# Layer 0, mixing weights: where the stride lies, in the matmul's read or in the copy's write

## Chip, cores, metric

The kernel runs on one core of one Trainium2 chip. The metric is device microseconds of one execution of the whole program; the reported time is the median of three executions.

## What is computed

The program is a chain of four layers on an image batch of 8 x 64 channels x 64 x 64. The change touches layer 0 alone, a spectral mixing layer (cut from the reference):

```python
z  = layernorm over channels(x) * ln_gamma + ln_beta
Xf = rfft2(z)                                             # 64 x 33 frequencies
Uf = Xf[:, :, None] * conj(phi_f)[None, None]             # 24 filters phi
U  = irfft2(Uf)
S  = einsum('bdlxy,lhd->bhxy', U, theta)
V  = einsum('hd,bdxy->bhxy', wv, S) + bv
G  = sigmoid(einsum('hd,bdxy->bhxy', wg, S) + bg)
return x + V * G
```

Filtering and the sum over filters and channels commute with the inverse transform. So the kernel forms, for every frequency, one mixing matrix from phi and theta, applies it to the spectrum, and transforms back once. Layers 1 to 3 (selective scans and convolutions) are the same before and after.

## The kernel before

Layer 0 runs in three stages, one after the other: `l0_forward` (normalise, transform along y), `l0_mix` (transform along x, mix, transform back along x) and `l0_back` (transform back along y, gate, add). Layer 1 follows. Inside the layer the order of work is the order of the code: each engine executes its own instructions in program order, and semaphores hold an instruction until its data or its buffer is ready.

`l0_mix` goes through the 33 values of ky in 17 pairs (the last pair holds one). For a pair there is one tile of mixing weights, `W`, of 128 partitions; partitions 0 to 63 multiply the real part of the input channels and 64 to 127 the imaginary part. Two such tiles exist, so the weights of the next pair are made while the present pair is applied. Four helpers share the work:

- `build(p)` makes `W` of pair p in 16 steps. A step runs four matmuls (line 692) into the two-bank PSUM tile `pw`, one for each of four output channels h; each gives 256 columns: two ky, real and imaginary (c), 64 values of kx. Then `evac` (lines 299 and 301) copies the 1024 columns out of PSUM. `evac` alternates: one copy on VectorE (line 299), the next on ScalarE (line 301), through all of its callers. There are two `pw` buffers, so the third step waits until the copy of the first has finished.
- `spectrum(p)` loads the input of a ky from DRAM (`yt`, line 708), transforms it (line 711, PSUM tile `q`) and scatters it into `xf` with two ScalarE and two VectorE instructions that take turns (lines 729 and 727). `xf` has kx outside and the batch inside, so that 8 columns of one kx lie together.
- `apply(p)` does the mixing. For each ky there are two halves of 32 kx each. A half is 32 matmuls (line 742) into the PSUM tile `ps`, of which there is one buffer. Four neighbouring kx go to four column tiles of the array, each 32 columns wide, and so to four groups of 32 PSUM partitions. The stationary operand is `xf` of that kx, the moving operand the 128 weights of that kx (2 c x 64 h). Then one `evac` to `so` and eight DMAs to DRAM (line 754).
- `inverse` transforms a finished ky back along x (line 766), with an `evac` to `o` and a DMA (line 769).

After each half of `apply` the code runs four steps of `build` for the next pair. So PE's order within a pair is: line 711 for the next pair, then four times (32 matmuls of line 742, then 16 matmuls of line 692), then line 766. A float32 matmul shows as two records in the trace: 64 records of line 742 in a half, and 8 of line 692 in a step.

The two accesses that the change swaps are the copy's output and the matmul's moving operand:

```python
W[p] = wp.tile([128, C, n], F32, name="W")                                  # h outside, (ky c kx) inside
o = W[p][:, 4 * m : 4 * m + 4, :].rearrange("p (r e) n -> p r (e n)", r=2)  # copy: contiguous
w = W[p].rearrange("p h (e c x) -> p e c h x", c=2, x=HW)[:, e]             # w[:, :, :, kx]: step n = 256 elements
```

Of the kernel before, what the change touches and what calls it, by code (L numbers as in the profile page):

```python
# [10 lines left out]
F32 = mybir.dt.float32  # L11
# [7 lines left out]
C = 64  # L19
HW = 64  # L20
# [248 lines left out]
class Net:  # L269
# [397 lines left out]
    def l0_mix(self, cp, wp, hy, hm, hs):  # L667

        nc, d = self.nc, self.d
        W2 = NB * C
        theta, phi, xdft, xinv, g, b = (self.load(cp, "l0_" + n) for n in ("theta", "phi", "xdft", "xinv", "g", "b"))
        for r in range(2):
            nc.scalar.mul(phi[r * 64 : r * 64 + NLAG, :, 1, :], phi[r * 64 : r * 64 + NLAG, :, 1, :], -1.0)

        nc.scalar.mul(b, b, float(L))
        pairs = [list(range(k, min(k + 2, KY))) for k in range(0, KY, 2)]
        W, xf, s2 = {}, {}, {}  # L680

        def build(p, pw_):

            kys = pairs[p]
            n = len(kys) * 2 * HW
            W[p] = wp.tile([128, C, n], F32, name="W")
            for m in range(C // 4):
                pw = pw_.tile([128, 2, 512], F32, name="pw")
                for e in range(2):
                    for r in range(2):  # L690
                        at = slice(r * 64, r * 64 + 2 * NLAG)
                        nc.tensor.matmul(
                            pw[:, r, e * n : e * n + n],
                            theta[at, 2 * m + e, :],
                            phi[at, kys[0] : kys[-1] + 1].rearrange("p k c x -> p (k c x)"),
                            start=True,
                            stop=True,
                        )
                o = W[p][:, 4 * m : 4 * m + 4, :].rearrange("p (r e) n -> p r (e n)", r=2)
                self.evac(o, pw[:, :, : 2 * n])  # L700
                yield

        def spectrum(p):

            for ky in pairs[p]:
                k, v = (ky % 32, 0 if ky % 32 else 1 + ky // 32)
                yt = tp.tile([128, W2], F32, name="yt")
                nc.sync.dma_start(yt, hy[k].rearrange("x s n -> (x s) n"))
                px = pq.tile([128, NP, 2, HW], F32, name="q")
                for q in range(NP):  # L710
                    nc.tensor.matmul(
                        px[:, q].rearrange("p c x -> p (c x)"),
                        yt[:, q * 128 : q * 128 + 128],
                        xdft[:, v].rearrange("p c x -> p (c x)"),
                        start=True,
                        stop=True,
                    )

                xf[ky] = tp.tile([128, (HW + 3) * NB], F32, name="xf", bufs=5)
                x = xf[ky].rearrange("p (x b) -> p b x", b=NB)  # L720
                nc.gpsimd.memset(x[:, :, HW:], 0.0)  # L721
                for i in range(2):
                    for c in range(2):
                        o = x[c * C : c * C + C, :, :HW].rearrange("p (q i) x -> p q i x", i=2)[:, :, i, :]
                        src_, scale = px[i * C : i * C + C, :, c, :], g[i * C : i * C + C]
                        if c:
                            nc.vector.tensor_scalar(o, src_, scale, None, ALU.mult)
                        else:
                            nc.scalar.activation(o, src_, AF.Copy, scale=scale)
                if ky == 0:  # L730
                    nc.vector.tensor_scalar(x[:C, :, 0], x[:C, :, 0], b[:C], None, ALU.add)

        def apply(p):
            for e, ky in enumerate(pairs[p]):
                w = W[p].rearrange("p h (e c x) -> p e c h x", c=2, x=HW)[:, e]
                x = xf.pop(ky)
                for half in range(2):
                    ps = ps_.tile([128, 8, 2, C], F32, name="ps")
                    for m in range(8):
                        for j in range(4):  # L740
                            kx = 4 * (half * 8 + m) + j
                            nc.tensor.matmul(  # L742
                                ps[32 * j : 32 * j + 32, m],
                                x[:, kx * NB : kx * NB + 32],
                                w[:, :, :, kx],
                                start=True,
                                stop=True,
                            )
                    so = tp.tile([128, 8, 2, C], F32, name="so")
                    self.evac(so, ps)  # L750
                    for j in range(4):
                        for c in range(2):
                            o = hm[ky, c].rearrange("(m j) b h -> j b m h", j=4)[j, :, half * 8 : half * 8 + 8, :]
                            nc.sync.dma_start(o, so[32 * j : 32 * j + NB, :, c, :])
                    yield

        def fetch(ky):
            s2[ky] = tp.tile([128, W2], F32, name="s2", bufs=4)
            nc.sync.dma_start(s2[ky], hm[ky].rearrange("c x b h -> (c x) (b h)"))

        def inverse(kys):

            po = pq.tile([128, W2], F32, name="q")
            for n, ky in enumerate(kys):
                v = 0 if ky % 32 else 1 + ky // 32
                nc.tensor.matmul(po, xinv[:, v, :], s2.pop(ky), start=n == 0, stop=n == len(kys) - 1)
            o = tp.tile([128, W2], F32, name="o")
            self.evac(o, po)
            nc.sync.dma_start(hs[:, :, kys[0] % 32, :].rearrange("x s n -> (x s) n"), o)


        with self.tc.tile_pool(name="l0pw0", bufs=2, space=PSUM) as pw_:
            for _ in build(0, pw_):
                pass
        yield

        with ExitStack() as ctx:
            own = lambda n, b, **k: ctx.enter_context(self.tc.tile_pool(name="l0m" + n, bufs=b, **k))
            tp, pw_, ps_, pq = own("t", 3), own("pw", 2, space=PSUM), own("ps", 1, space=PSUM), own("pq", 2, space=PSUM)
            spectrum(0)  # L780
            for p in range(len(pairs)):
                more = build(p + 1, pw_) if p + 1 < len(pairs) else iter(())
                if p + 1 < len(pairs):
                    spectrum(p + 1)
                back = [ky for ky in pairs[p - 2] if ky] if p > 1 else []
                for ky in back:
                    fetch(ky)
                for _ in apply(p):
                    for _ in range(4):
                        next(more, None)  # L790
                for _ in more:
                    pass
                for ky in back:
                    inverse([ky])
            for p in (len(pairs) - 2, ):
                for ky in pairs[p]:
                    fetch(ky)
                for ky in pairs[p]:
                    inverse([ky])
            fetch(0)  # L800
            fetch(KY - 1)
            inverse([0, KY - 1])
# [1347 lines left out]
```

## Time and profile before

| | us |
|---|---|
| median of 3 executions | 24766.56 (24764.24 to 24768.88) |
| span of the profiled execution | 24763.3 |
| layer 0, to about | 1128 |
| of it, mixing with weight building | 140 to 975 |
| first `build` (pair 0), ahead of `l0_forward` | 15.9 to 41 |

The profiled execution's span and the median differ by 3.3 us, which is 0.01%; what lies around the span is small. All times below in "us from the start" count from the start of the span. The page of the whole program is ruled by the scans of layers 1 to 3 (VectorE 91% and GpSimd 89% busy), and layer 0 is 4.6% of the span, so the views that matter are the ones cut to the window 140 to 975 us.

### The profile page before, as it was taken

The page shows a single profiled execution, that of the slowest core. Times are in us where ns is not written, and L with a number is a line of the kernel's source. Part 1 is how long each engine was busy: PE and PEld are TensorE (multiplying, and loading weights), DVE is VectorE, ACT ScalarE, POOL GpSimd, SP SyncE. Part 2 cuts the span into 40 slices and gives each one's busy share as a digit, 9 for nine tenths or more (in the row PEclk, how much of TensorE's full clock was granted, in tenths as well). Part 3 has the DMA queues.
Part 4 walks back from the last instruction along what each step waited for, and adds up shares of the span by engine and source line. Part 5 has one row for each costly group of instructions (what it writes and reads, how often), then busy time and mean ns, then how long its engine had stood idle before and what let it go on. Part 6 is the DMA issues. An engine that isn't in the chain of part 4 may idle for free. (4 is left out here: it accounts for less than half of the span.)

```text
span 24763.3 us, 192937 instructions
## 1 busy us (share of the span) xinstructions
PE 21205.6 (86%) x53146; PEld 8272.3 (33%) x53146; DVE 22452.5 (91%) x12956; ACT 14796.2 (60%) x18824; POOL 22125.0 (89%) x10580
## 2 busy tenths in 40 slices
PE   8877888888888888888888888888888888888888
PEld 6522333333333323322333333333333333333333
DVE  5399999999999779978999999999999999999999
ACT  4355555555555456624666666666666666666666
POOL 0199999999999669977999999999999999999999
PEclk9888999999999999999999999999999999999999
DMA  2399899898998669933555555555555555555554
GB/s 65 93 319 326 308 321 318 310 319 314 313 318 311 238 211 339 343 103 93 168 173 169 173 167 173 168 173 167 173 169 173 168 173 169 173 169 173 169 173 158
DMA packets 1835292, 5282.68 MB, mean 213 GB/s; under 512 B 533712, under 2 KB 539924, under 8 KB 1831904
## 3 DMA queue, kind: packets, MB, share of 16 engines
q1 hardware_dynamic: 1809632, 5207.00, 63.0%
q10 hardware_dynamic: 24576, 63.33, 0.7%
q8 instruction: 423, 6.93, 0.1%
q14 instruction: 661, 5.41, 0.1%
HBM read 5112.85 MB, written 156.11 MB: 213 GB/s over the span
## 5 line engine op out<-in xcount | busy, mean ns | idle before, releaser
L484 POOL TENSOR_TENSOR hb<-du,bc 128x1024 f32<-128x1024 f32 x4608 | 10746.4, 2360 | 204.5 <-DVE h L500 137.9
L306 PE MATMUL acc<-hc,ident 128*128 128x512 f32 x18560 | 8788.0, 614 | 87.6 <-DVE img L1266 49.9
L491 ACT ACTIVATE dA<-dt,w_A 128x512 f32<-128x512 f32 x8192 | 5673.1, 693 | 3923.3 <-DVE hc L514 2873.1
L500 DVE TENSOR_TENSOR_SCAN dA<-dA,hb 128x1024 f32<-128x1024 f32 x3320 | 7580.9, 2283 | 188.4 <-ACT dA L491 101.0
L306 PE MATMUL acc<-h,ident 128*128 128x512 f32 x8064 | 4652.9, 706 | 2430.0 <-POOL h L514 2400.9
L306 PEld LDWEIGHTS acc<-hc,ident 128*128 128x128 f32 x18560 | 3639.8, 200 | 5214.2 <-issue 4562.5
L484 POOL TENSOR_TENSOR hb<-du,b 128x1024 f32<-128x1024 f32 x2048 | 4919.7, 2476 | 467.4 <-DVE dA L500 205.6
L514 DVE TENSOR_TENSOR hc<-dA,bc 128x1024 f32<-128x1024 f32 x3232 | 3956.8, 1224 | 244.4 <-issue 4.5
L491 ACT ACTIVATE dA<-dt,w_l_A 128x1024 f32<-128x1024 f32 x2560 | 2863.6, 1119 | 1004.6 <-DVE hc L514 764.6
L500 DVE TENSOR_TENSOR_SCAN h<-dA,hb 128x1024 f32<-128x1024 f32 x1416 | 3229.1, 2280 | 82.0 <-ACT dA L491 80.2
L306 PEld LDWEIGHTS acc<-h,ident 128*128 128x128 f32 x8064 | 1569.1, 212 | 5155.8 <-POOL h L514 3484.1
L514 POOL TENSOR_TENSOR h<-h,bc 128x1024 f32<-128x1024 f32 x1376 | 3243.1, 2357 | 8.3 <-DVE h L500 8.3
L500 DVE TENSOR_TENSOR_SCAN dA<-dA,carry,hb 128x1024 f32<-128x1024 f32 x1320 | 3094.2, 2344 | 124.9 <-POOL hb L484 57.2
L514 DVE TENSOR_TENSOR hc<-dA,c 128x1024 f32<-128x1024 f32 x1408 | 1723.7, 1224 | 118.3 <-DMA c<-bc 7.2
L514 POOL TENSOR_TENSOR h<-h,c 128x1024 f32<-128x1024 f32 x640 | 1566.4, 2447 | 7.5 <-ACT carry L1249 6.9
L491 ACT ACT_TABLE_LOAD x1128 | 1447.2, 1283 | 19.7
L500 DVE TENSOR_TENSOR_SCAN h<-dA,carry,hb 128x1024 f32<-128x1024 f32 x600 | 1404.6, 2341 | 36.4 <-ACT dA L491 25.2
L1249 ACT COPY carry<-dA 128x1 f32<-128x1 f32 x1056 | 169.4, 160 | 1654.3 <-DVE hc L514 1613.4
L2004 PE MATMUL mm<-xn,taps 128*128 128x512 f32 x2048 | 932.9, 597 | 1.1 <-ACT z L2052 1.1
L721 POOL MEMSET xf<- 128x24 f32 x33 | 4.3, 141 | 851.4 <-PE ps L742 725.2
L2019 PE MATMUL mm<-u,w_xp 128*36 128x512 f32 x1024 | 489.8, 601 | 143.0 <-ACT u L2016 136.3
L2039 POOL TENSOR_TENSOR du<-dt,u 128x1024 f32<-128x1024 f32 x256 | 603.0, 2355 | 9.9 <-ACT dt L415 9.9
(320 smaller groups left out, 18494.0 us busy)
## 6 DMA issues: line engine op xcount, KB each, us to landing
bc<-bc SPq DMA_DIRECT2D x4096, 512.0 KB
b<-bc SPq DMA_DIRECT2D x2048, 512.0 KB
c<-bc SPq DMA_DIRECT2D x2048, 512.0 KB
bc<-bc SPq DMA_DIRECT2D x512, 1024.0 KB
tmp<-rs SPq DMA_DIRECT2D x93, 512.0 KB
raw<-x SPq DMA_DIRECT2D x64, 512.0 KB
inv<-rs SPq DMA_DIRECT2D x64, 512.0 KB
tmp<-x SPq DMA_DIRECT2D x192, 128.0 KB
```

What stands on the lines that cost most here:

```text
L306: self.nc.tensor.matmul(o, lhsT, r, start=start, stop=stop)
L484: nc.gpsimd.tensor_tensor(s.shaped(hb[i]), s.shaped(s.du), B.pop(i), ALU.mult)
L491: nc.scalar.activation(dA[i][:, cut], s.dt[:, cut], AF.Exp, scale=A[:, n : n + 1])
L500: nc.vector.tensor_tensor_scan(h[:, way], dA[i][:, way], hb.pop(i)[:, way], s.first(n), ALU.mult, ALU.add)
L514: engine.tensor_tensor(s.shaped(o), s.shaped(h), CC.pop(i), ALU.mult)
L721: nc.gpsimd.memset(x[:, :, HW:], 0.0)
L1249: nc.scalar.copy(self.carry[:, n : n + 1], h[:, last : last + 1])
L2004: nc.tensor.matmul(tokens(px[:, j * W : j * W + W]), w.taps[k][:, m, j * 128 : j * 128 + 128], xn[:, :, f : f + HW], start=m == 0, stop=m ...
L2019: nc.tensor.matmul(pd, w.xp[:, k, j, :], u[:, j * W : j * W + W], start=j == 0, stop=j == 1)
L2039: nc.gpsimd.tensor_tensor(du, dt, u, ALU.mult)
```

## The change

The weight tile is laid out with the 128 columns of one (ky, kx) side by side: `(ky kx)` outside, then c, then h. The matmul's moving operand becomes 128 consecutive elements. The copy out of PSUM reads the same 1024 columns in the same order as before and writes each to its new place: along kx its step is 128 elements, that is 512 bytes, and the four h of a step lie side by side. No instruction is added or removed; the tile has the same size.

```diff
-            W[p] = wp.tile([128, C, n], F32, name="W")
+            W[p] = wp.tile([128, n // 2, 2, C], F32, name="W")
+            into = W[p].rearrange("p (k x) c h -> p h k c x", x=HW)
...
-                o = W[p][:, 4 * m : 4 * m + 4, :].rearrange("p (r e) n -> p r (e n)", r=2)
-                self.evac(o, pw[:, :, : 2 * n])
+                o = into[:, 4 * m : 4 * m + 4]
+                if len(kys) == 2:
+                    self.evac(o, pw.rearrange("p r (e k c x) -> p (r e) k c x", e=2, k=2, x=HW))
+                else:
+                    ps = pw[:, :, : 2 * n].rearrange("p r (e c x) -> p r e c x", e=2, x=HW)
+                    self.evac(o[:, :, 0].rearrange("p (r e) c x -> p r e c x", r=2), ps)
...
-                w = W[p].rearrange("p h (e c x) -> p e c h x", c=2, x=HW)[:, e]
+                w = W[p].rearrange("p (k x) c h -> p k x c h", x=HW)[:, e]
...
-                                w[:, :, :, kx],
+                                w[:, kx],
```

## Prediction

> **What bounds the kernel now.** I first read the page: VectorE and GpSimd are busy 91% and 89% of the span, but in layers 1 to 3. Layer 0 runs alone ahead of them, so what its mixing stage gains or loses moves the end one for one. Then I read the busy time in the stretch of the mixing.
>
> ```profile
> core 0: us, PE busy (x) PEld busy (x) DVE busy (x) ACT busy (x) POOL busy (x), PEclk, DMA share, GB/s
> 140.00:975.00 835.00, 753.03 (x6561) 549.94 (x6554) 430.90 (x235) 365.48 (x234) 4.55 (x32) 0.96 0.17 38
> ```
>
> PE is busy 753 of 835 us; DMA is nearly idle. Of what, the groups by line of the same window say:
>
> ```profile
> L742 PE MATMUL ps<-W,xf 128*32 128x128 f32 x4224 | 430.5, 572 | 1.2 <-ACT so L301 1.2
> L299 DVE COPY W<-pw 128x1024 f32<-128x1024 f32 x120 | 295.2, 2460 | 135.8 <-PE pw L692 135.8
> L692 PE MATMUL pw<-w_l_phi,w_l_theta 48*128 48x256 f32 x1920 | 246.2, 392 | 22.0 <-DVE W L299 14.4 <-ACT W L301 7.5
> L301 ACT COPY W<-pw 128x1024 f32<-128x1024 f32 x120 | 228.6, 1905 | 177.3 <-PE pw L692 177.3
> ```
>
> The 4224 records of line 742 fill 430.5 us, 101.9 ns each; one of 66 halves takes 6.5 us. The copies idle waiting for PE, and PE waits for copies only 22 us. So PE sets the pace, line 742 first. The timeline of one half shows something else:
>
> ```profile
> 513.13 2.00 PE L692 MATMUL pw<-w_l_phi,w_l_theta 48*128 48x256 f32 x16 [0.46 <-DVE W L299]
> 514.31 3.44 DVE L299 COPY W<-pw 128x1024 f32<-128x1024 f32 x1 [1.24 <-PE pw L692]
> ...
> 515.05 6.58 PE L742 MATMUL ps<-W,xf 128*32 128x128 f32 x64
> 515.17 5.95 ACT L301 COPY W<-pw 128x1024 f32<-128x1024 f32 x1 [1.39 <-PE pw L692]
> ...
> 523.61 1.23 DVE L299 COPY W<-pw 128x1024 f32<-128x1024 f32 x1 [0.69 <-PE pw L692]
> ...
> 525.00 1.01 ACT L301 COPY W<-pw 128x1024 f32<-128x1024 f32 x1 [1.23 <-PE pw L692]
> ```
>
> The same copy takes 1.23 us on VectorE and 1.01 us on ScalarE beside line 692, but 3.44 and 5.95 us beside line 742. The strided reads hinder the writers of SBUF.
>
> **Prices in this trace.** Layer 1 reads one tile both ways: line 306, `mm<-u`, with a step of 64 elements (1415.99) and contiguous (1628.85). Its accumulator copy of 1024 columns has such a step in its output (line 1264).
>
> ```profile
> 1415.99 3.59 PE L306 MATMUL mm<-u,w_l_xp 128*68 128x512 f32 x4
> ...
> 1628.85 1.88 PE L306 MATMUL mm<-u,w_l_xp 128*68 128x512 f32 x4
> ```
>
> ```profile
> L1264 ACT COPY img<-acc x32: 1882/1912/1959, 1299.5 to 7825.1; 128x1024 f32<-128x1024 f32 x32
> ```
>
> The stride doubles a matmul's stream (3.59 against 1.88 us) and takes a ScalarE copy from 1.01 to 1.91 us. For VectorE, line 1266, which reads and writes its SBUF image, takes 1.21 us contiguous and 2.33 us strided; I take 2.25 us for a copy that only writes strided (estimate, bounds 1.23 and 2.33).
>
> **What the Trainium skill says.** "SBUF — State Buffer", Specifications: lines of 16 bytes, at least two hits per line for full bandwidth. The pairs above agree: a factor of about two, on both the reading and the writing side. The same page, Who interferes with whom, says that PE and ACT never wait on anyone; the ScalarE copy at 5.95 us beside line 742 against 1.01 us disagrees, and I go by the trace. "TensorE: Matmul & The Clock Gate", Part 3: matmuls in different column tiles run concurrently. The trace agrees for two 64-column tiles (24 records of line 376 in 5.37 us, 224 ns each, against 1.88/4 = 470 ns in the row above); for four 32-column tiles no row shows the contiguous rate.
>
> **The change, part by part.**
>
> *Reads of line 742 become contiguous.* By the factor of two, 101.9 ns becomes 51 ns: 4224 x 51 = 215 us, **215 us less**. Bounds: a record of 128 contiguous columns on the full array takes 111 ns (line 634: 8 records in 1.05 us, of which about 0.27 is the last one's own latency); four tiles side by side could bring 28 ns, 117 us in all, 313 less. At the other end nothing changes. A check of the middle: the densest short contiguous records are 16 of line 692 at 128 columns in 1.16 us, 59 ns each less latency.
>
> *Copies of `W` scatter.* 1.23 becomes 2.25 us, 1.01 becomes 1.91 us. They ran hidden beside PE; the cover fails in one place. Two steps of `build` take PE 1.92 us (513.13 to 515.05), one 0.96, and there are two `pw` buffers. Counted from the first matmul of line 692 in a half (510.67 in this trace): the copy of step 0 starts at 1.18 (511.85), that of step 1 at 2.10 (ScalarE, 512.77). With VectorE first, step 0's copy ends at 3.43; step 2, waiting for it, runs 3.47 to 4.43; step 3, whose buffer is free at 4.01, follows to 5.39. With ScalarE first, step 2 runs 3.13 to 4.09 and step 3 waits for VectorE's copy, 4.39 to 5.35. Today this takes 4.38 us (510.67 to 515.05). **+1.0 us a half**; the 60 halves that build a full pair lose 60 us, the four that build the single ky about 2. Bounds: 0, were scatter free; 60 us more for every further microsecond of a copy.
>
> Behind those copies on VectorE and ScalarE stand the copy of `ps` and, at the pair's turn, those of `q`. The last two copies of a half end at about 6.9 and 7.8; the next half's `build` wants their buffers only after line 742, at 5.4 + 3.3 = 8.7. That is still covered, and line 742 will hinder them less, having a quarter of the lines to fetch per column; if it hinders them as today, that is the slower rival below.
>
> *What is late next.* At a pair's start eight instructions of lines 729 and 727 run in turn, 0.72 us each when undisturbed: 5.8 us from 1.5 us ahead of line 742. Today they hide under its 6.5 us. With 3.3 us they end about 1 us after it, and the copies of `ps` and of step 0 queue behind: 1.5 us x 15 pairs = **+22 us** (bounds 0 and 40). At a pair's end, `o`, its DMA (line 769) and the `yt` load behind it in SP's queue wait for the last scattered copy: about 0.4 us x 15 = **+6 us**. SP's eight DMAs of line 754 take 2.7 us of a half of 8.7 us; SP and the POOL memsets stay off the path.
>
> *The first build*, ahead of `l0_forward`, alternates step and copy: every VectorE chain of step, copy, step grows by 1.02 us, eight in a row: **+8 us** (bounds 0 and 16).
>
> *Sum.* -215 + 60 + 2 + 22 + 6 + 8 = -117 us against the profiled execution: a span of 24646 from 24763.3, and with the 3.3 us that the median stands above it **24650 us**. 0.2%, about what a measurement of this kernel can tell from no change, is 50 us.
>
> **Rivals.**
>
> *Four tiles stream at full rate.* For it: two 64-column tiles do. Line 742 falls to 117 us; the `q` copies show by another 24 us in all. -313 + 98 + 24 = -191: 24576 us.
>
> *Something else paces short matmuls.* In line 376 at 64 columns, contiguous, 12 records take 1.23 us, about 84 ns each less latency; and the half at 967.80, with no copy beside it, still takes 6.29 us, so the copies are not what slows line 742. If weight loads or issue hold a record at 84 ns, the gain is 4224 x 17.9 = 76 us and the sum -76 + 98 = +22: 24789 us. It breaks even at 79 ns a record; if the read's stride is not the limit at all, +98: 24865 us. Against: the same array does 59 ns in line 692.
>
> *The slower case: scattered copies dominate.* Place: step 2 of each four, waiting for step 0's copy. Price: 60 us per microsecond of copy. The sum of -117 is used up at 117/60 = 1.95 us more, a copy of about 4.2 us. That is what copies take today beside line 742 (VectorE mean 2.46, single ones 5.95). Against: the copy that step 2 waits for runs beside line 692, which leaves today's copies at 1.23 and 1.01 us. At 5.5 us the sum is 3.25 x 60 - 117 = +78: 24845 us. [...]lines 729 and 727 step by 32 bytes, line 1264 by 256, and both pay near 0.9 ns an element.
>
> That the change doesn't do what it says is excluded: the moving operand's address pattern is contiguous by construction.
>
> **How the numbers follow.** Likeliest case 0.57, its own range 24603 to 24680 (40 to 58 ns a record). Full-rate tiles 0.15. Paced by something else 0.13, half of it near zero and half slower. Scattered copies dominate 0.07. Mixtures 0.08, a quarter of it faster and the rest near zero. So faster 0.57 + 0.15 + 0.02 = 0.74, same 0.12, slower 0.14. The range 24560 to 24785 takes in the first rival and most of the near-zero cases, and leaves out about 0.15 above and a little below.
>
> **What would show it.** Right: line 742 near 215 us busy and 3.3 us a half; ScalarE copies of `W` near 1.91 and VectorE near 2.25 us, with few over 4; idle time of line 692 behind `W` grown from 22 to about 80 us; line 299's wait for `pw` smaller. Wrong: line 742 above 75 ns a record, copies of 4 us beside line 692, or a moved time in layers 1 to 3, whose instructions should keep their durations.

## The result, and the profile after

The median fell from 24767.72 us (four runs, 24764.24 to 24779.97) to **24524.1 us** (four runs, 24510.87 to 24533.47). The ratio is 0.9901, with a 95% interval from 0.9887 to 0.9915. The profiled execution took 24525.61 us; its span is 24523.8 us against 24763.3, 239.5 us less. The direction was forecast, but the gain is twice the 117 us of the prediction, and the median lies 36 us below its range.

In the changed kernel the lines have moved: `build`'s matmul is line 693, the mixing matmul 747, `spectrum`'s matmul 716 with its copies 734 and 732. The groups by line, cut to the mixing (140 to 800 us), show busy time, mean ns of one instruction, and the idle time of the engine ahead of the group with what ended it:

```profile
L693 PE MATMUL pw<-w_l_phi,w_l_theta 48*128 48x256 f32 x1920 | 243.2, 393 | 69.0 <-DVE W L299 34.7 <-ACT W L301 34.3
L301 ACT COPY W<-pw 128x1024 f32<-128x1024 f32 x120 | 231.3, 1927 | 126.0 <-PE pw L693 126.0
L299 DVE COPY W<-pw 128x1024 f32<-128x1024 f32 x120 | 230.6, 1922 | 116.3 <-PE pw L693 115.8
L747 PE MATMUL ps<-W,xf 128*32 128x128 f32 x4224 | 143.4, 293 | 1.2 <-ACT so L301 1.2
```

Three things are to be seen. The mixing matmul fell from 430.5 to 143.4 us, 33.9 ns a record (143.4 / 4224), where 51 were forecast. The copies take 1.92 us on both engines, 2.04 us at the longest, whatever runs beside them. And `build` now waits 69.0 us for them, against 22.0 before: the copies have come onto the path, as forecast, but for less.

The timeline of one half shows the order behind it:

```profile
306.69 2.06 PE L693 MATMUL pw<-w_l_phi,w_l_theta 48*128 48x256 f32 x16 [1.11 <-DVE W L299]
307.87 1.97 DVE L299 COPY W<-pw 128x1024 f32<-128x1024 f32 x1 [1.24 <-PE pw L693]
308.67 1.96 PE L747 MATMUL ps<-W,xf 128*32 128x128 f32 x64
308.79 2.00 ACT L301 COPY W<-pw 128x1024 f32<-128x1024 f32 x1 [1.23 <-PE pw L693]
310.56 2.00 PE L693 MATMUL pw<-w_l_phi,w_l_theta 48*128 48x256 f32 x16
...
312.60 1.89 DVE L299 COPY W<-pw 128x1024 f32<-128x1024 f32 x1 [0.68 <-PE pw L693]
313.67 2.01 PE L693 MATMUL pw<-w_l_phi,w_l_theta 48*128 48x256 f32 x16 [1.12 <-ACT W L301]
```

A half's 64 records take 1.96 us where they took 6.58. The ScalarE copy beside them takes 2.00 us, where it took 5.95. Before the third step of `build` PE stands idle for 1.1 us, until the scattered copy of the first step gives its buffer back: that is the new wait of the prediction, in its place. From one half to the next it is now 6.94 us (308.67 to 315.61). It was 10.91 (515.05 in the prediction's timeline to this line of the kernel before):

```profile
525.96 6.42 PE L742 MATMUL ps<-W,xf 128*32 128x128 f32 x64
```

The mixing stage (first to last record of the mixing matmul) shrank from 834.4 us (139.6 to 974.0) to 585.5 us. In the busy time by stretch, it is the last row shown:

```profile
core 0: us, PE busy (x) PEld busy (x) DVE busy (x) ACT busy (x) POOL busy (x), PEclk, DMA share, GB/s
0.00:51.80 51.80, 31.61 (x129) 19.62 (x129) 15.80 (x13) 20.51 (x12) 0.70 (x6) 1.00 0.43 153
...
155.00:740.50 585.50, 456.86 (x6559) 351.79 (x6558) 328.72 (x235) 324.36 (x234) 3.98 (x28) 0.94 0.24 54
```

The first `build` ends at 51.8 us where it ended at 41.1. Layers 1 to 3 kept their times within some 13 us each, in both directions.

### The profile page after: what moved, and what is told of

It is laid out like the page before. It is cut to its first block, busy times and chain, and to the rows that moved or that the text cites. A ratio compares the mean times of both kernels' runs of the same rounds, so it can differ in the third digit from the quotient of the medians.

```text
span 24523.8 us, 192937 instructions
## 1 busy us (share of the span) xinstructions
PE 20916.6 (85%) x53146; PEld 8080.3 (33%) x53146; DVE 22352.9 (91%) x12956; ACT 14733.5 (60%) x18824; POOL 22093.4 (90%) x10580
## 3 DMA queue, kind: packets, MB, share of 16 engines
q10 hardware_dynamic: 24576, 63.33, 0.7%
## 5 line engine op out<-in xcount | busy, mean ns | idle before, releaser
L484 POOL TENSOR_TENSOR hb<-du,b 128x1024 f32<-128x1024 f32 x2048 | 4834.2, 2390 | 490.5 <-DVE dA L500 215.9
L514 DVE TENSOR_TENSOR hc<-dA,bc 128x1024 f32<-128x1024 f32 x3232 | 3954.9, 1224 | 244.7 <-issue 4.9
L514 DVE TENSOR_TENSOR hc<-dA,c 128x1024 f32<-128x1024 f32 x1408 | 1722.9, 1224 | 116.8 <-DMA c<-bc 6.9
```

The source lines that it names most:

```text
L484: nc.gpsimd.tensor_tensor(s.shaped(hb[i]), s.shaped(s.du), B.pop(i), ALU.mult)
L514: engine.tensor_tensor(s.shaped(o), s.shaped(h), CC.pop(i), ALU.mult)
```

## The experiments

The result left one large question. The trace said that a stride doubles a matmul's stream, and the matmul became three times faster. Either four column tiles reading contiguous data side by side gain more than the one tile on which the factor was read, or the old reads paid for something beside the stride. The smaller question was what the scattered copies cost.

The times of pad_step, one_tile_before, one_tile_after, runs_of_4, runs_of_2 and both_stride are of one execution each. Four executions of one kernel lie up to 27 us apart here, so these six are read from the lengths of their instructions, and not from small differences of the whole time.

### pad_step: the stride kept, its length changed

This is the kernel before with rows of `W` four elements longer, so that the matmul reads at a step of 1040 bytes in place of 1024. The copies stay contiguous. Three small tiles (`yo`, `o`, `s`) get two buffers to make room.

```diff
-            W[p] = wp.tile([128, C, n], F32, name="W")
+            W[p] = wp.tile([128, C, n + 4], F32, name="W")
...
```

> The kernel before with the row of W lengthened from 256 to 260 elements, so the moving operand of line 742 steps by 1040 bytes and not by 1024 (to make room, yo, o and s have two buffers in place of three). Theory line (every moving column fetches its own 16-byte line, and the four column tiles share the fetches): the step's size does not matter, line 742 stays at 90 to 105 ns a record, 380 to 440 us busy. Rival bank (a step of a power of two sends all fetches to one bank): line 742 falls below 60 ns a record, under 250 us busy, and the program ends at least 100 us sooner than before.

It took 24601.33 us, against 24765.69 for the kernel before on the same chip: 16 bytes of padding per row bring two thirds of the gain. (The mixing begins 7 us later than before, at 146.7 us against 139.6; whether the smaller pools are the cause is not known.) The groups by line, and then the copies of `W` in the view by tile (shortest, median, longest duration in ns), of this kernel:

```profile
L742 PE MATMUL ps<-W,xf 128*32 128x128 f32 x4224 | 255.7, 409 | 1.1 <-ACT so L301 1.1
```

```profile
L299 DVE COPY W<-pw x136: 680/1224/1226, 19.9 to 794.8; 128x1024 f32<-128x1024 f32 x128, 128x512 f32<-128x512 f32 x8
L301 ACT COPY W<-pw x136: 585/1012/1017, 21.6 to 794.1; 128x1024 f32<-128x1024 f32 x128, 128x512 f32<-128x512 f32 x8
```

A record takes 60.5 ns of busy time (255.7 / 4224), just above the 60 ns that the rival named, and 55 from start to start inside a half, where it was 95. There is no slow copy left: the longest is 1.23 us, against 6.86 and 7.09 us before. So the 101.9 ns were two costs. The stride itself about doubles the stream, as the prediction had it (55 against 26.7 ns from start to start in the changed kernel); the step of 1024 bytes costs another factor of about 1.7 (101.9 / 60.5), and it is this second cost that came with the slow copies. The theory that each column pays for its own 16-byte line and nothing else, under which the padding changes nothing, fell. What in the memory the reads at 1024 bytes collide on, no run shows; "collision" stands here for the measured loss alone.

### one_tile_before, one_tile_after: the same reads, one tile at a time

The two loops of a half are exchanged, so that eight kx of one column tile follow one another and the four tiles no longer run side by side.

```diff
-                    for m in range(8):
-                        for j in range(4):
+                    for j in range(4):
+                        for m in range(8):
```

> The kernel before with the loops over m and j of a half exchanged: eight matmuls in a row go to the same column tile, so no neighbours run side by side. Values are the same. By line 306's strided row (857 ns for 512 columns) a record takes 214 ns alone. Theory (four strided streams at a step of 1024 bytes obstruct each other): the rate of before, 95 ns, is far from 214/4 = 54, and one tile at a time takes 200 to 220 ns. Rival (column tiles never ran side by side in this kernel, and 95 ns is the price of one stream): it stays at 95 to 110 ns.

> The changed kernel with the same exchange of loops. One contiguous stream of 128 columns: 107 to 111 ns a record if tiles don't overlap, four times the 27 ns of the changed kernel. Against one_tile_before it gives the stride's factor for a single 32-column tile: 2 by the theory. Rival (something else than column tiles side by side gave the changed kernel its 27 ns): it stays near 30 ns.

They took 25090.38 and 24792.37 us. Groups by line of the first, then of the second:

```profile
L742 PE MATMUL ps<-W,xf 128*32 128x128 f32 x4224 | 755.5, 393 | 1.1 <-ACT so L301 1.1
...
L299 DVE COPY W<-pw 128x1024 f32<-128x1024 f32 x120 | 146.9, 1224 | 403.7 <-PE pw L692 403.7
L301 ACT COPY W<-pw 128x1024 f32<-128x1024 f32 x120 | 121.4, 1012 | 444.3 <-PE pw L692 444.3
```

```profile
L747 PE MATMUL ps<-W,xf 128*32 128x128 f32 x4224 | 405.8, 279 | 1.1 <-ACT so L301 1.1
```

One tile after another, a record takes 178.9 ns strided and 96.1 ns contiguous (busy time / 4224): the factor is 1.86. Both lie below what was expected, because at a change of tile the two tiles overlap for some records. Inside one tile the records start 216 and 109 ns apart, as expected: a factor of 1.98, the "factor of two" of the prediction.

Side by side, by busy time, the contiguous records gain 96.1 / 33.9 = 2.8 over this, the padded stride gains 178.9 / 60.5 = 3.0, and the step of 1024 bytes only 178.9 / 101.9 = 1.8. From start to start it is plainer: four contiguous tiles side by side take 26.7 ns a record (109 / 4 = 27), four padded ones 55 (216 / 4 = 54), so they run at four times the rate of one; at the step of 1024 bytes they take 95. The collision thus shows where four tiles read at once at that step; with one tile at the same step the copies are undisturbed too (1224 and 1012 ns). The Trainium skill, "TensorE: Matmul & The Clock Gate", Part 3, lists a measured speedup of 3.07 for four row tiles; here four column tiles show 2.8 by busy time, and 4.1 from start to start (109 / 26.7), which is more. The last pair, which holds one ky and so has a step of 512 bytes, was as slow (6.29 us for 64 records in the kernel before).

### runs_of_4, runs_of_2: how much of a line must be used

In these the layout lies between the two: q neighbouring h are together, then the columns, then the groups of h. The matmul reads runs of 16 or of 8 bytes at steps of 4096 or 2048 bytes; the copy writes single elements 16 or 8 bytes apart.

```diff
-            W[p] = wp.tile([128, C, n], F32, name="W")
+            W[p] = wp.tile([128, C // 4, n, 4], F32, name="W")     # runs_of_2: C // 2, n, 2
...
```

> W laid out [h/4][ky c kx][4 h]: the moving operand reads runs of 4 elements, one full 16-byte line each, at a step of 4096 bytes; the copy writes with a step of 16 bytes. Theory line: 32 fetches in place of 128 for a record, so line 742 runs at the full rate of the changed kernel, 27 to 30 ns a record. Rival bank or rival that only consecutive lines are fast: it stays above 60 ns. Copies of W: with one element to a line as in the changed kernel, 1.88 us on both engines if the price is one line for each write; if only large steps cost, 1.23 and 1.01 us.

> W laid out [h/2][ky c kx][2 h]: runs of 2 elements, 8 bytes of a line, at a step of 2048 bytes. Theory line: 64 fetches for a record, half of before, 45 to 55 ns a record. Rival (two hits on a line are enough for full rate, as the skill's SBUF page says): 27 to 30 ns.

They took 24545.28 and 24508.81 us (before on the same chip: 24765.69). Groups by line of runs_of_4, then of runs_of_2:

```profile
L299 DVE COPY W<-pw 128x1024 f32<-128x1024 f32 x120 | 240.6, 2005 | 117.0 <-PE pw L692 116.5
L301 ACT COPY W<-pw 128x1024 f32<-128x1024 f32 x120 | 240.4, 2004 | 130.1 <-PE pw L692 130.1
...
L742 PE MATMUL ps<-W,xf 128*32 128x128 f32 x4224 | 145.0, 295 | 1.2 <-ACT so L301 1.2
```

```profile
L742 PE MATMUL ps<-W,xf 128*32 128x128 f32 x4224 | 167.1, 313 | 1.2 <-ACT so L301 1.2
L299 DVE COPY W<-pw 128x1024 f32<-128x1024 f32 x120 | 150.3, 1253 | 131.2 <-PE pw L692 130.8
...
L301 ACT COPY W<-pw 128x1024 f32<-128x1024 f32 x120 | 136.4, 1137 | 161.6 <-PE pw L692 161.2
```

Reading whole 16-byte lines is as good as contiguous (145.0 against 143.4 us), at a step of 4096 bytes at that. Reading half lines costs 24 us more, 39.6 ns a record; the 45 to 55 ns of a theory of one fetch for each line were too many, and the 27 to 30 ns of its rival, from start to start, were a little too few (35 inside a half, from 2.52 us for 64 records). On the writing side, elements 16 bytes apart cost the same as elements 512 bytes apart (2.00 and 1.92 us), and elements 8 bytes apart nearly nothing (1.25 and 1.14 us). So, at the steps tried, a write is slow where it fills one element of a line at a time, and how far apart the lines lie matters little. This agrees with the Trainium skill, "SBUF — State Buffer", Specifications: two hits in a line for full bandwidth. VectorE's writes reach it with two, ScalarE's and the matmul's reads nearly.

### both_stride: the scattered copies alone

The changed kernel's copies, with the mixing matmul reading at the old step of 1024 bytes (and so other elements than it needs).

```diff
-                w = W[p].rearrange("p (k x) c h -> p k x c h", x=HW)[:, e]
+                w = W[p].rearrange("p y c h -> p (y c h)").rearrange("p (h e c x) -> p e c h x", h=C, c=2, x=HW)[:, e]
...
```

> The copies scatter as in the changed kernel, but line 742 reads at a step of 256 elements as before (it reads other elements of the tile, so the values are not those of the reference). Theory line: line 742 stays near 100 ns a record; copies of W take 1.9 us beside line 692 but compete with line 742 for lines and take 6 us and more beside it; the build steps stretch by the same 0.7 us a half as in the changed kernel: about 60 us slower than before, 24830 us. Rival (the writes, not the reads, are what the stride of before made expensive): line 742 changes by over 20 ns a record.

It took 24836.43 us, 71 us more than the kernel before. Groups by line:

```profile
L747 PE MATMUL ps<-W,xf 128*32 128x128 f32 x4224 | 437.6, 582 | 1.2 <-ACT so L301 1.2
L693 PE MATMUL pw<-w_l_phi,w_l_theta 48*128 48x256 f32 x1920 | 243.4, 393 | 67.7 <-DVE W L299 34.2 <-ACT W L301 33.5
L299 DVE COPY W<-pw 128x1024 f32<-128x1024 f32 x120 | 226.2, 1885 | 204.8 <-PE pw L693 204.8
```

The wait of `build` is 67.7 us, 46 more than before, as in the changed kernel. One reading was not expected by any theory: beside the colliding reads (103.6 ns a record) the scattered copies keep their 1.88 us (none over 1.92), where in the kernel before the contiguous copies on VectorE grew to between 2.6 and 6.9 us and some on ScalarE to 7.1. Why the one is slowed and the other not is open.

### no_stride: neither side strided

The kernel before with its contiguous copies, and the matmul reading 128 consecutive elements of the tile (others than it needs).

```diff
-                w = W[p].rearrange("p h (e c x) -> p e c h x", c=2, x=HW)[:, e]
+                w = W[p].rearrange("p h n -> p (h n)").rearrange("p (k x c h) -> p k x c h", x=HW, c=2, h=C)[:, e]
...
```

> The kernel before with its contiguous copies, and line 742 reading 128 consecutive elements of the tile (others than it needs: the values are not those of the reference). This is the change without the cost of its scattered copies. Expected by all theories: line 742 at 27 to 30 ns a record, copies of W at 1.23 and 1.01 us even beside it, build steps of a half at 4.4 us, a half at 6.4 us, the program at 24475 us. The difference to the changed kernel, some 50 us, is what scattering costs; the prediction had 98 us for it.

It took 24484.2 us (24480.32 to 24495.76), a ratio to the kernel before of 0.9883 (0.9867 to 0.99). Groups by line:

```profile
L692 PE MATMUL pw<-w_l_phi,w_l_theta 48*128 48x256 f32 x1920 | 246.8, 393 | 26.4 <-DVE W L299 18.3 <-ACT W L301 8.1
...
L742 PE MATMUL ps<-W,xf 128*32 128x128 f32 x4224 | 137.5, 285 | 1.2 <-ACT so L301 1.2
```

It is the floor for this change: the scatter costs the changed kernel 40 to 50 us (24524.1 and 24534.32 in its two sets of runs), made of the wait of `build` (69.0 against 26.4 us) and of the first `build`, which ends here at 40.4 us, 11 us sooner; other groups of the changed kernel are a few us shorter and give some of it back.

### h_inner: the same layout, written a line at a time

The changed kernel, with the loops of the copy's access pattern in another order: h is innermost, so that the four h of a step are written one after the other into one 16-byte line. PSUM is read at a step of 1024 bytes instead.

```diff
-                    self.evac(o, pw.rearrange("p r (e k c x) -> p (r e) k c x", e=2, k=2, x=HW))
+                    o = W[p].rearrange("p (k x) c h -> p k c x h", x=HW)[:, :, :, :, 4 * m : 4 * m + 4]
+                    self.evac(o, pw.rearrange("p r (e k c x) -> p k c x (r e)", e=2, k=2, x=HW))
```

> The changed kernel with the same copy walked in another order: h innermost. It now writes the four h of a step, one full 16-byte line, one after the other, and reads PSUM at a step of 256 elements for them. Theory (a scattered copy pays for the second visit to a line, on the SBUF side): copies of W fall to 1.23 us on VectorE and 1.01 on ScalarE, the first build ends near 41 us, a half takes 6.4 us in place of 6.94, and the program 24475 us. Rival (the strided PSUM read costs the same): copies stay at 1.9 us or more and the time at 24525 us or above.

It took **24493.07 us** (24486.11 to 24498.41), a ratio to the kernel before of 0.9885 (0.987 to 0.99): each of its four runs is below each of the eight runs of the changed kernel, the fastest of which took 24510.87 us, and they overlap with those of no_stride. The forecast was 24475. Groups by line:

```profile
L693 PE MATMUL pw<-w_l_phi,w_l_theta 48*128 48x256 f32 x1920 | 249.4, 396 | 28.6 <-DVE W L299 19.9 <-ACT W L301 8.7
...
L299 DVE COPY W<-pw 128x1024 f32<-128x1024 f32 x120 | 146.9, 1224 | 131.7 <-PE pw L693 131.2
L748 PE MATMUL ps<-W,xf 128*32 128x128 f32 x4224 | 140.2, 289 | 1.2 <-ACT so L301 1.2
L301 ACT COPY W<-pw 128x1024 f32<-128x1024 f32 x120 | 121.5, 1012 | 160.0 <-PE pw L693 159.9
```

The copies are back at 1.22 and 1.01 us, to the nanosecond those of contiguous to contiguous. So the price of the scatter was in its order and not in its layout, and reading PSUM at a step costs these copies nothing.

### h_inner_early: the next wait taken away

What is late next in h_inner is the input of `spectrum` at a pair's end (its matmul waits 65.4 us in all for `yt`, as it did before the change, 64.7). Here each `yt` is loaded one pair sooner.

```diff
+                    early(p + 2)          # dma_start of yt for the pair after the next
...
-                yt = tp.tile([128, W2], F32, name="yt")
-                nc.sync.dma_start(yt, hy[k].rearrange("x s n -> (x s) n"))
+                yt = yts.pop(ky)
```

> h_inner, and the loads of yt for a pair issued one pair earlier, right after the transforms of the pair before (line 708's DMA now stands ahead of the last DMAs of a pair in SP's queue). In h_inner PE stands still about 4 us at each of some 15 pair ends (line 771 ends near 307.0, line 717 starts at 311.1), waiting for the load that was queued behind the store of o. Theory: that wait goes, 4 us x 15 = 60 us, 24435 us. Rival (the transforms of the next pair then only wait for the copies of q, or for the q buffers that o still holds): under 20 us of it shows, 24475 us or more.

It took 24506.33 us (24499.49 to 24526.08), a ratio of 0.9891 (0.9874 to 0.9907): no gain over h_inner (which ran on a different chip). The wait for `yt` did go, from 65.4 to 7.4 us. But `build` now idles 87.9 us and the mixing matmul fills 162.9. The timeline of two halves, and the busy time by stretch around them (PEclk, the granted clock, is the third figure from the right):

```profile
320.11 2.64 PE L693 MATMUL pw<-w_l_phi,w_l_theta 48*128 48x256 f32 x16 [1.77 <-DVE W L299]
322.68 2.93 PE L754 MATMUL ps<-W,xf 128*32 128x128 f32 x64
325.54 2.00 PE L693 MATMUL pw<-w_l_phi,w_l_theta 48*128 48x256 f32 x16
327.78 1.14 PE L693 MATMUL pw<-w_l_phi,w_l_theta 48*128 48x256 f32 x8 [0.25 <-ACT W L301]
330.03 1.14 PE L693 MATMUL pw<-w_l_phi,w_l_theta 48*128 48x256 f32 x8 [1.11 <-ACT W L301]
331.09 1.95 PE L754 MATMUL ps<-W,xf 128*32 128x128 f32 x64
```

```profile
311.00:318.00 7.00, 7.00 (x100) 5.47 (x98) 3.69 (x5) 3.40 (x5) 0.00 (x0) 1.00 0.62 197
318.00:330.00 12.00, 8.90 (x108) 6.39 (x104) 5.59 (x5) 5.04 (x6) 0.14 (x1) 0.86 0.22 38
```

The last step of the second half shown waits 1.11 us for a copy, which it does not do in h_inner. The idle time of PE in the mixing stage is thus about what it was (96.5 us, 90.7 in h_inner): a stall was traded for other stalls. Beside this PE ran slower more often. The first half shown takes 2.93 us, in a stretch with a clock of 0.86, and the clock records of the trace stand at half speed for 112.6 us of the stage, against 79.0 in h_inner; PE's busy time there grew by 25 us (488.7 against 464.0). The traced execution is the slowest of the four. Whether the new gaps bring the lower clock is not shown: the 1.95 us right behind the gap of 1.11 are at the usual speed. The rival that less than 20 us would show had the number right, but for another reason; why the fourth step came to wait for the copy of the third was not found.

### after_again: the changed kernel once more

> The changed kernel once more, on the chip of the next run: 0.990 of before, 24520 to 24535 us. No theory says otherwise; it fixes what h_inner gains over it (about 0.13%) on one chip.

It took 24534.32 us (24526.33 to 24535.6), a ratio of 0.9902 (0.9887 to 0.9917), on the chip of h_inner_early. The result stands. Against h_inner, which ran on a different chip, the medians differ by 31 and 41 us in the two sets of runs, while the intervals of the ratios still touch (0.987 to 0.99 and 0.9887 to 0.9917).

## Why the prediction was wrong, point by point

**The reads: the step that failed.** "Reads of line 742 become contiguous. By the factor of two, 101.9 ns becomes 51 ns: 4224 x 51 = 215 us" was the mis-sized term. It measured 143.4 us busy, 287 less. The factor itself was right (1.86 with one tile at a time, 1.98 from start to start), but it was applied to a number that held a second factor of about 1.7: what four tiles reading at once at a step of 1024 bytes lose. The price of line 306 came from one stream, at a step of 256 bytes, and one stream shows no second factor even at 1024 bytes (one_tile_before). What could have warned is in the prediction: the strided reads slowed the two copies about three- and sixfold (3.44 against 1.23 us, 5.95 against 1.01). A plain doubling of the stream doesn't do that, as pad_step showed later. It was noted, and no price was drawn from it.

**The first rival had the mechanism.** "Four tiles stream at full rate" gave 117 us for line 742, and 26.7 ns a record are seen from start to start inside a half. It was given a chance of 0.15, although two 64-column tiles in this same trace already showed the gain. Its 117 us were too few for the busy time, 143.4: 64 records take 1.96 us with the time of the last one, which makes 129 us for 66 halves, and 16 halves ran slower than that. Its time, 24576 us, was too high all the same, because it carried the costs of the copies of the likeliest case, 98 us, and 24 more for the `q` copies.

**The copies.** ScalarE's 1.91 us was right (1.93). VectorE's estimate of 2.25 was too high (1.92): line 1266, its upper bound, also reads SBUF at a step, and the estimate stayed close to it. That steps of 512 bytes cost about what those of 256 do held: 0.90 ns an element on ScalarE ((1.93 - 1.01) / 1024) against 0.88 for line 1264. The same 0.9 for lines 729 and 727 had no contiguous copy of their size to rest on. The new wait is where it was put, before the third step. In the 60 halves that build a full pair it comes to 47 us (69.0 less 22.0), where the prediction had 82 for it: 60 for the steps, 22 for the `q` copies at a pair's start. The four steps of a half in the middle of a pair take 5.12 us against 4.46, so they pay about 0.7 us where 1.0 was forecast. In the first half of a pair PE waits 1.25 us in the mean, 0.13 more than in the others, where 1.5 was forecast on top: the `q` copies cost almost nothing. Nor do the 6 us for the pair's end show: the wait for `yt` is 62.9 us, and it was 64.7.

**The first build.** 10.7 us against 8. The longer copies alone would have given 8 x (1.89 - 1.23) = 5.3 us; what was missed is PE. Timeline of the first `build` of the changed kernel, then a line of the kernel before:

```profile
25.65 3.79 PE L693 MATMUL pw<-w_l_phi,w_l_theta 48*128 48x256 f32 x16 [0.26 <-DVE W L299]
...
29.73 3.80 PE L693 MATMUL pw<-w_l_phi,w_l_theta 48*128 48x256 f32 x16 [0.28 <-DVE W L299]
```

```profile
30.60 2.09 PE L692 MATMUL pw<-w_l_phi,w_l_theta 48*128 48x256 f32 x16 [0.16 <-DVE W L299]
```

Sixteen records take 3.80 us, nearly twice the 2.00 of the mixing stage, through the whole first `build`. Before the change single records fall from 631 to 376 ns at about 27.7 us, and from then on sixteen take 2.0 to 2.1. The Trainium skill, "TensorE: Matmul & The Clock Gate", Part 1, says that PE starts at half rate and is released by a few microseconds of sustained activity. The traces agree on the two rates. The activity took longer here: before the change PE worked for over 9 us almost without a gap (17.92 to 27.4) until it was released. In the changed kernel it idles 0.26 to 0.28 us behind every second copy and was not released in 30 us. That these gaps are the reason fits, and was not tested by itself. The PEclk column shows 1.00 here only because the clock records of the trace begin later, at 57.1 us, and at 27.7 in the kernel before.

**The sum.** 287 less for the reads, 47 more for the waits and 11 for the first `build` make 229 less; the span shows 239.5. The other 10 us are several small things. Inside the mixing stage PE's busy time fell by 296 us (753.03 to 456.86), so other matmuls gave 9. Between the first `build` and the mixing some 5 us were lost (the mixing starts 15.3 us later, not 10.7), and behind the mixing some 6 were gained, with layers 1 to 3 moving both ways.

**The rivals that fell.** "Something else paces short matmuls" at 84 ns is excluded by 26.7 ns. The slower case, scattered copies of over 4 us, is excluded: the longest took 2.04 us. That copies would be hindered less by contiguous reads was right, and more so than said: 1.88 us alone, 2.00 us beside line 747.

## What to carry to other kernels

Where matmuls in several column tiles read a strided moving operand, try another step, or runs of at least 8 bytes, before giving up contiguous copies: here 1040 bytes for 1024, 16 bytes of padding a row, brought 164 us of the 284 of h_inner. Steps of single elements other than 512, 1024 and 1040 bytes were not tried. When a layout must be changed in the copy out of PSUM, put the loop that fills a 16-byte line innermost and let the PSUM side take the stride. And a factor read from one stream must not be applied to a row in which several streams run at once, above all if that row also slows its neighbours.

## What was not expected of the hardware

- Four column tiles reading at a step of 1024 bytes take 101.9 ns a record, at 1040 bytes 60.5, contiguous 33.9. A single tile at 1024 bytes pays only the factor of two (216 against 109 ns from start to start); at 1040 bytes a single tile was not run.
- Under that collision, contiguous copies on VectorE and ScalarE grow from 1.23 and 1.01 us to as much as 6.86 and 7.09, while scattered ones keep their 1.88 us. This is open.
- Copies of 1024 elements into SBUF take 1.23 and 1.01 us contiguous, 1.25 and 1.14 us at a step of 8 bytes, 2.00 us at 16 and 1.92 us at 512.
- Reading PSUM at a step of 1024 bytes adds nothing to these copies (1.22 and 1.01 us).
